# A graph layer's scatter sum on one core: a 256-column window per tile, or 16 slots per tile placed eight tiles at a time

## The chip, the core and the metric

The kernel runs on one core of one Trainium2 chip. The metric is device microseconds of one execution, taken without the profiler; the median of several executions counts. The profile is a separate execution, with the profiler on, and is read for where the time goes. Engines are named as the profile names them: PE is TensorE (PEld is its weight load), DVE is VectorE, ACT is ScalarE, POOL is GpSimd, SP is SyncE.

## What is computed

Two layers of a relational graph convolution over 12,500 nodes with 128 features, 200,000 edges sorted by their destination, and 8 relations. A residual sum and a normalisation over the features follow. Cut to what matters:

```python
def _rgcn_conv(x, src, dst, et, basis, comp, root, bias):
    W = jnp.einsum('rb,bio->rio', comp, basis)
    xw = jnp.einsum('ni,rio->nro', x, W)
    msgs = xw[src, et]                                   # a row for every edge
    seg = dst * N_REL + et
    summed = segment_sum(msgs, seg, N_NODES * N_REL)
    cnt = segment_sum(ones, seg, N_NODES * N_REL)
    mean = summed / jnp.maximum(cnt, 1.0)[:, None]
    agg = mean.reshape(N_NODES, N_REL, HIDDEN).sum(axis=1)
    return agg + x @ root + bias

h = x
for l in range(2):
    h = relu(_rgcn_conv(h, src, dst, et, basis[l], comp[l], root[l], bias[l])) + h
out = layernorm(x + h)
```

## The kernel before

**Tiles, quads and groups.** The 200,000 edges are cut into T = 1563 tiles of 128 edges, in their sorted order. Four tiles make a quad (Q = 4, NQ = 391 quads), eight tiles make a group (G = 8, NG = 196 groups). Nodes go in blocks of 128 (NT = 98 blocks). Because the edges are sorted and the graph has 16 edges for each node on average, a tile's destinations lie within K = 16 neighbouring nodes of the tile's first one, and the destinations of a group of 8 tiles lie in a window of 256 nodes. Where an input does not allow this, a general path behind a branch (line 1287) is taken; it is not taken here.

**Layer 1** (loop at line 1187) gathers the rows of `x` for the edges: `gather`, line 603, one indirect DMA of POOL for each tile, 128 rows of 512 bytes each, four DMAs a quad. `onehot` (line 894) makes for each tile a matrix of 128 edges by 128 columns (8 relations by 16 slots) on DVE: it compares the constant row `cols`, which lies in PSUM, with the edge's own column and multiplies by the edge's weight 1/count. `means` (line 954) multiplies the gathered rows with it, `product` (line 975) applies the 8 relation matrices and leaves 8 tiles x 16 slots = 128 rows of `y`, ACT copies these to `ys` (line 591), and `place` (line 1008) adds them to the window of 256 nodes with a 128x256 matrix of ones and zeros that `place_in` (line 986) makes on DVE from `pos`, the place of every slot. `finish` (lines 1024, 1041, 1042) adds the part carried over from the window before and the bias, applies relu and the residual, and leaves a block of 128 nodes, transposed, in `hT`. `table` (line 1054) multiplies that block with the 8 relation matrices of layer 2 and stores the products to `y_d` in HBM.

**Layer 2** (loop at line 1235) gathers rows of `y_d`, one for each edge, in the same way (line 603, 1563 indirect DMAs of 128 rows). A row is a finished message here, so it is only weighted and summed. `onehot` makes for each tile a matrix of 128 edges by 256 columns, again from `cols`, comparing with `near`, the edge's place in the 256-node window. `add_rows` (line 1091) multiplies the tile's rows, as the stationary operand, with that matrix and accumulates straight into the window of 256 nodes, for about 16 tiles; at the first tile of a window one more matmul adds `h @ root` (line 1094). `finish` then takes the block off, and after every eighth block `norm` turns it back (line 1113), adds `x`, normalises (lines 1119 to 1132) and stores it, in pieces that the list `todo` spreads over the next quads, one piece a quad.

**Order.** No scheduler reorders anything. Each engine executes its instructions in the order of the calls, and the class `Plan` inserts the semaphore waits: a read waits for the write, a new write waits for the readers of the buffer. POOL's queue holds little but the gathers. The gather of quad q + 12 (AHEAD) is issued before quad q is summed, into a ring of 14 buffers (`rows_r`, line 541), so it waits until PE has read quad q - 2; it also waits until the gather three quads earlier has landed (three semaphore lanes, line 571). `onehot` runs two quads ahead in a ring of four (`dm_r`, line 542). The first gather of layer 2 waits for all of `y_d`.

**Preparation.** `counts` (lines 706 to 773) runs once for the first block of 128 tiles before the first quad, and three times for four blocks each during the first quads of layer 1. It makes the tables that `onehot` and `gather` read; `near` is the last of them: one DVE instruction for each block (line 760), transposes on PE (line 767), a copy on ACT.

Of the kernel before, what the change touches and what calls it, by code (L numbers as in the profile page):

```python
# [10 lines left out]
I32 = mybir.dt.int32  # L11
# [404 lines left out]
def ordered_path(  # L416
# [67 lines left out]
    w = keep([P, B * P], F32, "w")  # L484
    near = keep([P, B * P], F32, "near")
    pos = keep([P, B, 2 * R], F32, "pos")
# [40 lines left out]
    def h_cells(j):  # L527
# [7 lines left out]
    small = {n: keep([P, 1], t, n) for n, t in (  # L535
        ("nb_i", I32), ("nb_n", F32), ("p_in", I32), ("p_inf", F32), ("p_g", I32), ("p_gf", F32),
        ("p_r", I32), ("p_rf", F32))}
# [3 lines left out]
    rows_r = Ring(const, AHEAD + 2, [P, Q, D], F32, "rows")  # L541
    dm_r = Ring(const, 4, [P, Q, 2 * P], F32, "dm")
    sT_r = Ring(const, 3, [P, R, G, K], F32, "sT")
# [162 lines left out]
    def counts(i):  # L706
# [51 lines left out]
        nr, nc_ = turns.take()  # L758
        for b in range(b0, b1):
            vec(lambda b=b: nc.vector.tensor_scalar(nr[:, b - b0], dx[:, b, main], small["nb_n"],  # L760
                                                    float(-b * P * G), op0=ALU.subtract, op1=ALU.add),
                dxc + ["nb_n"], [nc_ + (b - b0,)])
        pt, pc = pt_b

        def emit():
            for b in range(nb):
                last = nc.tensor.transpose(pt[:, b, :], nr[:, b, :], ident)
            return last

        pe(emit, [nc_ + (b,) for b in range(nb)] + ["ident"], [pc, nc_])  # L770
        copy(near[:, b0 * P:b1 * P], pt[:, :nb, :].rearrange("p b t -> p (b t)"), [pc],
             [("near", b) for b in range(b0, b1)])
        yield
# [111 lines left out]
    def onehot(l, q):  # L885
        if q >= NQ:
            return
        t, cell = dm_r.take()
        dms[l, q] = (t, cell)
        wide, ids = (P, kr) if l == 0 else (2 * P, near)  # L890

        def emit():
            for i in range(q * Q, q * Q + in_quad(q)):
                last = nc.vector.tensor_scalar(t[:, i - q * Q, :wide], cols[:, :wide], ids[:, i:i + 1],  # L894
                                               w[:, i:i + 1], op0=ALU.is_equal, op1=ALU.mult)
            return last

        b = q * Q // P
        vec(emit, ["cols", ("kr" if l == 0 else "near", b), ("wt", b)], [cell])

# [87 lines left out]

    def place(g):

        m = tiles_of(g) * K
        t, c = pl.pop(g)
        o, oc = ys.pop(g)
        k = two_blocks(g)
        opens = g == 0 or two_blocks(g - 1) != k
        last = g == NG - 1 or two_blocks(g + 1) != k
        if opens:
            b, bc = po_b[k % 2]
            acc[k] = b.rearrange("p t d -> p (t d)")[:, :2 * P], bc
        a, ac = acc[k]  # L1000
        root_in = opens and k >= 0
        reads = [c, oc]
        if root_in:
            xt, xc = x_cols(k)
            reads += xc + [("w", 0, R)]

        def emit():
            ins = nc.tensor.matmul(a, o[:m], t[:m], start=opens, stop=last and not root_in)  # L1008
# [38 lines left out]
    def table(j):  # L1047
# [4 lines left out]
        def half(k):  # L1052
# [12 lines left out]
            elif k == 1:  # L1065
# [7 lines left out]

    acc_b = [(s_b[0][0].rearrange("p t d -> p (t d)")[:, :2 * P], s_b[0][1]),
             (s_b[1][0].rearrange("p t d -> p (t d)")[:, :2 * P], s_b[1][1]),
             (ct_b[0].rearrange("p t d -> p (t d)")[:, :2 * P], ct_b[1])]

    def add_rows(q, k, opens, last):
        t, c = rows_g.pop((1, q))
        d, dc = dms.pop((1, q))  # L1080
        a, ac = acc[k]
        n = in_quad(q)
        root_in = opens and k >= 0
        reads = [c, dc]
        if root_in:
            ht, hc = hT[:, k * P:k * P + rows_of(k)], ("h", k)
            reads += [hc, ("w", 1, R)]

        def emit():
            for i in range(n):  # L1090
                ins = nc.tensor.matmul(a, t[:, i, :], d[:, i, :], start=(opens and i == 0),  # L1091
                                       stop=(last and i == n - 1))
                if i == 0 and root_in:
                    nc.tensor.matmul(a[:, :rows_of(k)], w_sb[:, 1, R, :], ht, start=False, stop=False)
            return ins

        pe(emit, reads, [ac])

    def norm(n, h):
# [4 lines left out]
        xt, xc = xs[n]  # L1104
        b, bc = po_b[h]
        st, sc = st_r.take()
# [34 lines left out]

    def sup(q):
        return (q * Q + G) // (2 * G) - 1


    def run(gen, n):
# [9 lines left out]
    vec(lambda: nc.vector.memset(ones, 1.0), [], ["ones"])  # L1156
    vec(lambda: nc.vector.tensor_single_scalar(small["nb_i"], part, G, op=ALU.add), ["part"], ["nb_i"])
    vec(lambda: nc.vector.tensor_single_scalar(small["nb_i"], small["nb_i"], 4, op=ALU.logical_shift_right), [], ["nb_i"])
    vec(lambda: nc.vector.tensor_copy(small["nb_n"], small["nb_i"]), ["nb_i"], ["nb_n"])
    vec(lambda: nc.vector.tensor_scalar(small["nb_n"], small["nb_n"], float(P), float(-P), op0=ALU.mult, op1=ALU.add),  # L1160
        [], ["nb_n"])
    copy(cols, iota_f, ["iota"], ["cols"])
# [24 lines left out]
    for q in range(NQ - 1):  # L1187
# [8 lines left out]
        if q % 2 == 0:  # L1196
            if g > 0:
                product(g - 1)
        elif g > 0:
            place(g - 1)  # L1200
# [19 lines left out]
    means(NQ - 1)  # L1220
    place(g - 1)
    todo.pop(0)()
    product(g)
    todo.pop(0)()
    place(g)
    while todo:
# [89 lines left out]
```

## Time and profile before

| what | value |
|---|---|
| median of 3 executions | 3990.28 us |
| lowest and highest | 3987.99 us, 3999.04 us |
| profiled execution, its own time | 4626.96 us |
| its span, first to last instruction | 4625.2 us |
| mean granted TensorE clock | 0.741 |
| layer 1: first to last gather | 3.5 to 2333.1 us |
| layer 2: first to last gather | 2378.4 to 4584.9 us |
| PE busy | 2403.7 us, 52% |
| DVE busy | 1652.6 us, 36% |
| ACT busy | 495.7 us, 11% |
| POOL busy | 2962.3 us, 64% |
| DMA engines, mean busy share, from the rows of the 40 slices | 0.1 to 0.3 |

The profiled execution is 637 us longer than the median of the others. A reader has to keep this in mind: a wait that stands in the profile need not stand in an ordinary execution. A line of the table of groups reads: source line, engine, operation, what is written from what, shape, count | busy time and mean of one | idle time of the engine just before such instructions, and what ended most of it. "issue" is idle time that ended without a wait that the profile shows, "remote" idle time ended by something that the profile could not name.

### The profile page before, as it was taken

Reading aid. Unit: us, or ns where it says so; the run is one execution under the profiler, and the core shown is the slowest. Engines: PE = TensorE matmul, PEld = TensorE weight load, DVE = VectorE, ACT = ScalarE, POOL = GpSimd, SP = SyncE. Lnnn points to the kernel's source line nnn. Section 1 sums busy time; section 2 is a strip of 40 time slices with the busy share of each in tenths; the row PEclk is TensorE's granted clock in tenths of the full one; section 3 lists DMA queues with packets and bytes.
Section 4 is the critical chain, followed back from the end, with each engine's and each line's share of the span. In section 5 each row is a group of like instructions: output and inputs, shape, how many; then the busy total and the mean of one; then the engine's idle time right before and its main releaser. Section 6 shows DMA issues by size and latency. Waiting matters only on the chain.

```text
span 4625.2 us, 32936 instructions
## 1 busy us (share of the span) xinstructions
PE 2403.7 (52%) x11205; PEld 1929.6 (42%) x11205; DVE 1652.6 (36%) x4580; ACT 495.7 (11%) x1042; POOL 2962.3 (64%) x3134
## 2 busy tenths in 40 slices
PE   1675655555655655565572454354445453444444
PEld 1454554454545544454452333333333342333333
DVE  3764322222322222222232334343334343333344
ACT  0121211112112212121110000000000000000000
POOL 5466666666666666666646666666666666666664
PEclk9897778777777778777786676666666666676776
DMA  3122222222222222222221121112122121221211
GB/s 85 33 64 73 74 73 69 73 69 73 69 73 74 73 69 74 69 73 66 73 70 45 48 56 55 48 54 57 46 57 55 47 56 45 56 58 45 58 51 38
DMA packets 128275, 282.52 MB, mean 61 GB/s; under 512 B 53327, under 2 KB 60763, under 8 KB 128099
## 3 DMA queue, kind: packets, MB, share of 16 engines
q0 software_dynamic: 100032, 205.07, 17.0%
q1 hardware_dynamic: 25546, 73.59, 4.3%
q10 hardware_dynamic: 2521, 1.66, 0.1%
q8 instruction: 92, 1.51, 0.1%
q14 instruction: 84, 0.69, 0.0%
HBM read 222.51 MB, written 57.60 MB: 61 GB/s over the span
## 4 chain that ended last, share of the span: by engine, by line
another core or an unknown queue 43%; PE 27%; issue 13%; DVE 13%; ACT 3%; POOL 2%; DMA 0%; POOLq 0%; DVEq 0%; ACTq 0%; SPq 0%
DVE dm L894 8%; PE s L954 8%; PE y L975 7%; PE pt L1054 4%; PE po L1008 3%; POOL rows L603 2%; PE ct L1091 2%; ACT sT L591 1%; PE s L1091 1%; PE ct L732 1%; DVE w_sb L623 1%; PE ct L733 1%; DVE arena L726 1%; ACT carry L1024 1%
## 5 line engine op out<-in xcount | busy, mean ns | idle before, releaser
L603 POOL DMA_INDIRECT rows<-in_x_dram,idx x1563 | 1485.2, 950 | 846.9 <-issue 417.3
L603 POOL DMA_INDIRECT rows<-y_d,idy x1563 | 1476.0, 944 | 775.8 <-issue 442.4
L1091 PE MATMUL s<-dm,rows 128*128 128x256 f32 x2086 | 672.0, 479 | 811.2 <-DVE dm L894 518.4
L894 DVE TENSOR_SCALAR dm<-cols,near,w 128x256 f32<-128x256 f32 x1563 | 725.6, 533 | 829.6 <-remote 686.4
L1091 PEld LDWEIGHTS s<-dm,rows 128*128 128x128 f32 x2086 | 491.1, 245 | 958.6 <-DVE dm L894 570.5
L894 DVE TENSOR_SCALAR dm<-cols,kr,w 128x128 f32<-128x128 f32 x1563 | 525.4, 401 | 493.4 <-remote 324.1
L954 PEld LDWEIGHTS s<-dm,rows 128*128 128x128 f32 x3126 | 485.1, 224 | 138.2 <-issue 113.3
L1008 PE MATMUL po<-pl,ys 128*128 128x256 f32 x392 | 168.8, 521 | 698.0 <-ACT ys L591 566.9
L975 PE MATMUL y<-w_sb,sT 128*128 128x128 f32 x3136 | 463.3, 310 | 95.0 <-issue 54.9
L954 PE MATMUL s<-dm,rows 128*128 128x128 f32 x3126 | 492.9, 307 | 20.4 <-issue 19.2
L1091 PE MATMUL ct<-dm,rows 128*128 128x256 f32 x1040 | 334.2, 478 | 325.2 <-DVE dm L894 187.0
L975 PEld LDWEIGHTS y<-w_sb,sT 128*128 128x128 f32 x3136 | 442.8, 225 | 110.7 <-issue 63.4
L1091 PEld LDWEIGHTS ct<-dm,rows 128*128 128x128 f32 x1040 | 245.9, 245 | 395.5 <-DVE dm L894 213.3
L1008 PEld LDWEIGHTS po<-pl,ys 128*128 128x128 f32 x392 | 74.3, 237 | 728.9 <-ACT ys L591 590.4
L1041 DVE TENSOR_TENSOR v<-po,carry 128x128 f32<-128x128 f32 x98 | 28.5, 291 | 932.2 <-ACT carry L1024 782.3
L591 ACT ACTIVATE sT<-s 128x512 f32<-128x512 f32 x391 | 233.7, 598 | 758.3 <-PE s L954 412.6
L1054 PE MATMUL pt<-w_sb,arena 128*128 128x512 f32 x388 | 239.8, 705 | 21.0 <-issue 8.9
L1024 ACT ACTIVATE carry<-s,bias_t 128x128 f32<-128x128 f32 x65 | 23.9, 368 | 1321.4 <-remote 1026.3
L591 ACT ACTIVATE y_row<-pt 128x512 f32<-128x512 f32 x194 | 115.7, 596 | 258.9 <-PE pt L1054 80.9
L591 ACT ACTIVATE ys<-y 128x128 f32<-128x128 f32 x196 | 54.2, 277 | 756.0 <-remote 526.8
L732 PE MATMUL ct<-arena,id_h 128*128 128x512 f16 (+1 forms) x188 | 70.9, 397 | 94.4 <-DVE arena L726 65.4
L1041 DVE TENSOR_TENSOR v<-s,carry 128x128 f32<-128x128 f32 x66 | 18.9, 286 | 274.8 <-ACT carry L1024 152.4
(121 smaller groups left out, 978.2 us busy)
## 6 DMA issues: line engine op xcount, KB each, us to landing
y_d<-y_row SPq DMA_DIRECT2D x96, 512.0 KB
rows<-in_x_dram,idx POOLq DMA_INDIRECT x1563
rows<-y_d,idy POOLq DMA_INDIRECT x1563
x_g<-in_x_dram SPq DMA_DIRECT2D x24, 512.0 KB
out_dram<-x_g SPq DMA_DIRECT2D x12, 512.0 KB
arena<-in_L_gnn_basis_dram SPq DMA_DIRECT2D x2, 512.0 KB
arena<-in_dst_dram ACTq DMA_DIRECT2D x2, 448.0 KB
arena<-in_edge_type_dram SPq DMA_DIRECT2D x2, 448.0 KB
```

The lines of the kernel that those rows point to most:

```text
L591: act(lambda: nc.scalar.activation(out_t, in_t, AF.Copy), reads, writes)
L603: return [nc.gpsimd.indirect_dma_start(out=t[:, i - q * Q, :], out_offset=None, in_=x if l == 0 else y_d, in_offset=bass.IndirectOffsetOnA ...
L623: vec(lambda b=b: nc.vector.scalar_tensor_tensor(w_sb[:, l, r, :], b_sb[:, l, b, :], comp_sb[:, c0 + b:c0 + b + 1], w_sb[:, l, r, :], op0= ...
L732: nc.tensor.matmul(ct[:, :nb, :], id_h, eq[:, s - s0, :nb, main], start=(s == 1), stop=False)
L894: last = nc.vector.tensor_scalar(t[:, i - q * Q, :wide], cols[:, :wide], ids[:, i:i + 1], w[:, i:i + 1], op0=ALU.is_equal, op1=ALU.mult)
L954: last = nc.tensor.matmul(s[:, i, :], t[:, i, :], d[:, i, :P], start=True, stop=True)
L975: last = nc.tensor.matmul(y[:m], t[:, r, :nt, :].rearrange("p t k -> p (t k)"), w_sb[:, 0, r, :], start=(r == 0), stop=(r == R - 1))
L1008: ins = nc.tensor.matmul(a, o[:m], t[:m], start=opens, stop=last and not root_in)
L1024: act(lambda: nc.scalar.activation(nt, a[:, P:], AF.Identity, bias=bias_t[:, l:l + 1]), [ac, ("bias_t", l)], [ncell])
L1041: vec(lambda: nc.vector.tensor_add(v[:, :n], a[:, :n], t[:, :n]), [ac, c], [vc])
L1054: pe(lambda: nc.tensor.matmul(hb[:n].rearrange("p r d -> p (r d)"), hT[:, j * P:j * P + n], w_sb[:, 1, k * H:(k + 1) * H, :].rearrange("p ...
L1091: ins = nc.tensor.matmul(a, t[:, i, :], d[:, i, :], start=(opens and i == 0), stop=(last and i == n - 1))
```

## The change

Layer 2 sums as layer 1 does, in two steps in place of one. `onehot` makes a matrix of 32 columns for each tile in place of 256: it compares with `slot`, the distance of the edge's destination from the tile's first destination, plus 16 for tiles of odd number. `sums` takes the place of `add_rows`: now the 32-column matrix is the stationary operand and the gathered rows (128 columns) are the moving one; two neighbouring tiles accumulate into the same 32 partitions, one using the first 16 and the other the last 16, so that 8 tiles fill 128 partitions of a PSUM bank (`y` for even groups, the first quarter of `ct` for odd ones). After the second quad of a group ACT copies the bank to `ys`. `place_in` makes the matrix of places as in layer 1, and `place`, which now takes the layer as an argument, adds the group's 128 slots to the window of 256 nodes one group later, in the banks `po`, with the root's matmul at the opening of a window. `norm` takes the banks `s` in place of `po`. What followed the last `add_rows` of a window (`finish`, and the start of `norm`) follows `place` now. In `counts`, `slot` is made with two DVE instructions for all blocks of a call (a subtraction of two arrays, then an addition of `odd`) in place of one instruction for each block.

The number of matmuls for the sum itself stays at one for each tile. Gathers, their order and the rings' depths are the same; `dm_r` has half the width.

```diff
@@ -533,13 +533,13 @@
...
-    dm_r = Ring(const, 4, [P, Q, 2 * P], F32, "dm")
+    dm_r = Ring(const, 4, [P, Q, P], F32, "dm")
...
@@ -756,20 +756,11 @@
         turned("DVE", idy, "idy", iy, ic, b0, b1)
         yield
         nr, nc_ = turns.take()
-        for b in range(b0, b1):
-            vec(lambda b=b: nc.vector.tensor_scalar(nr[:, b - b0], dx[:, b, main], small["nb_n"],
-                                                    float(-b * P * G), op0=ALU.subtract, op1=ALU.add),
-                dxc + ["nb_n"], [nc_ + (b - b0,)])
-        pt, pc = pt_b
-
-        def emit():
-            for b in range(nb):
-                last = nc.tensor.transpose(pt[:, b, :], nr[:, b, :], ident)
-            return last
-
-        pe(emit, [nc_ + (b,) for b in range(nb)] + ["ident"], [pc, nc_])
-        copy(near[:, b0 * P:b1 * P], pt[:, :nb, :].rearrange("p b t -> p (b t)"), [pc],
-             [("near", b) for b in range(b0, b1)])
+        vec(lambda: nc.vector.tensor_tensor(nr[:, :nb], dx[:, bs, main],
+                                            dx[:, bs, HALO:HALO + 1].to_broadcast([P, nb, P]), op=ALU.subtract),
+            dxc, [nc_])
+        vec(lambda: nc.vector.tensor_scalar(nr[:, :nb], nr[:, :nb], small["odd"], None, op0=ALU.add), ["odd"], [nc_])
+        turned("ACT", slot, "slot", nr, nc_, b0, b1)
         yield
 
     def where():
...
@@ -887,16 +878,16 @@
             return
         t, cell = dm_r.take()
         dms[l, q] = (t, cell)
-        wide, ids = (P, kr) if l == 0 else (2 * P, near)
+        m, ids = (P, kr) if l == 0 else (2 * K, slot)
 
         def emit():
             for i in range(q * Q, q * Q + in_quad(q)):
-                last = nc.vector.tensor_scalar(t[:, i - q * Q, :wide], cols[:, :wide], ids[:, i:i + 1],
+                last = nc.vector.tensor_scalar(t[:, i - q * Q, :m], cols[:, :m], ids[:, i:i + 1],
                                                w[:, i:i + 1], op0=ALU.is_equal, op1=ALU.mult)
             return last
 
         b = q * Q // P
-        vec(emit, ["cols", ("kr" if l == 0 else "near", b), ("wt", b)], [cell])
+        vec(emit, ["cols", ("kr" if l == 0 else "slot", b), ("wt", b)], [cell])
 
 
     def shape_of(n):
...
@@ -986,7 +977,7 @@
...
-    def place(g):
+    def place(l, g):
...
@@ -1001,20 +992,20 @@
         root_in = opens and k >= 0
         reads = [c, oc]
         if root_in:
-            xt, xc = x_cols(k)
-            reads += xc + [("w", 0, R)]
+            xt, xc = x_cols(k) if l == 0 else (hT[:, k * P:k * P + rows_of(k)], [("h", k)])
+            reads += xc + [("w", l, R)]
 
         def emit():
             ins = nc.tensor.matmul(a, o[:m], t[:m], start=opens, stop=last and not root_in)
             if root_in:
-                ins = nc.tensor.matmul(a[:, :rows_of(k)], w_sb[:, 0, R, :], xt, start=False, stop=last)
+                ins = nc.tensor.matmul(a[:, :rows_of(k)], w_sb[:, l, R, :], xt, start=False, stop=last)
             return ins
 
         pe(emit, reads, [ac])
         if last:
-            n = finish(0, k)
+            n = finish(l, k)
             if n is not None:
-                table(k)
+                table(k) if l == 0 else norms(k)
 
     def finish(l, k):
 
...
@@ -1071,30 +1062,36 @@
     todo = []
 
 
-    acc_b = [(s_b[0][0].rearrange("p t d -> p (t d)")[:, :2 * P], s_b[0][1]),
-             (s_b[1][0].rearrange("p t d -> p (t d)")[:, :2 * P], s_b[1][1]),
-             (ct_b[0].rearrange("p t d -> p (t d)")[:, :2 * P], ct_b[1])]
-
-    def add_rows(q, k, opens, last):
+    sum_b = [y_b, ct_b]
+
+    def sums(q):
         t, c = rows_g.pop((1, q))
         d, dc = dms.pop((1, q))
-        a, ac = acc[k]
+        g = q * Q // G
+        y, yc = sum_b[g % 2]
+        y = y if g % 2 == 0 else y[:, 0, :]
         n = in_quad(q)
-        root_in = opens and k >= 0
-        reads = [c, dc]
-        if root_in:
-            ht, hc = hT[:, k * P:k * P + rows_of(k)], ("h", k)
-            reads += [hc, ("w", 1, R)]
 
         def emit():
             for i in range(n):
-                ins = nc.tensor.matmul(a, t[:, i, :], d[:, i, :], start=(opens and i == 0),
-                                       stop=(last and i == n - 1))
-                if i == 0 and root_in:
-                    nc.tensor.matmul(a[:, :rows_of(k)], w_sb[:, 1, R, :], ht, start=False, stop=False)
-            return ins
-
-        pe(emit, reads, [ac])
+                j = (q * Q + i) % G // 2 * 2 * K
+                last = nc.tensor.matmul(y[j:j + 2 * K, :], d[:, i, :2 * K], t[:, i, :], start=(i % 2 == 0),
+                                        stop=(i % 2 == 1 or i == n - 1))
+            return last
+
+        pe(emit, [c, dc], [yc])
+        if q % 2 == 1 or q == NQ - 1:
+            m = tiles_of(g) * K
+            o, oc = ys[g] = ys_r.take()
+            copy(o[:m], y[:m], [yc], [oc])
+
+    def norms(k):
+        n = k // S
+        if k % S == S - 1 or k == NT - 1:
+            for h in range(-(-shape_of(n)[1] // 4)):
+                norm(n, h)
+            if n + 2 < NX:
+                todo.append(lambda: load_x(n + 2))
 
     def norm(n, h):
 
...
@@ -1102,7 +1099,7 @@
...
-        b, bc = po_b[h]
+        b, bc = s_b[h]
...
@@ -1233,26 +1225,20 @@
     for q in range(2):
         onehot(1, q)
     for q in range(NQ):
-        k = sup(q)
+        g = q * Q // G
         gather(1, q + AHEAD)
         if q + AHEAD == NQ - 1:
             pool(lambda: nc.gpsimd.drain())
         onehot(1, q + 2)
-        opens = q == 0 or sup(q - 1) != k
-        last = q == NQ - 1 or sup(q + 1) != k
-        if opens:
-            acc[k] = acc_b[k % 3]
-        add_rows(q, k, opens, last)
+        if q % 2 == 0 and g > 0:
+            place_in(g - 1)
+        sums(q)
+        if (q % 2 == 1 or q == NQ - 1) and g > 0:
+            place(1, g - 1)
         if todo:
             todo.pop(0)()
-        if last:
-            finish(1, k)
-            n = k // S
-            if k >= 0 and (k % S == S - 1 or k == NT - 1):
-                for h in range(-(-shape_of(n)[1] // 4)):
-                    norm(n, h)
-                if n + 2 < NX:
-                    todo.append(lambda n=n: load_x(n + 2))
+    place_in(NG - 1)
+    place(1, NG - 1)
     while todo:
         todo.pop(0)()
 
```

More of the change, by code (lines that the diff above doesn't have):

```diff
@@ L484, in ordered_path @@
     w = keep([P, B * P], F32, "w")
-    near = keep([P, B * P], F32, "near")
+    slot = keep([P, B * P], F32, "slot")
     pos = keep([P, B, 2 * R], F32, "pos")
@@ L535, in ordered_path @@
     small = {n: keep([P, 1], t, n) for n, t in (
-        ("nb_i", I32), ("nb_n", F32), ("p_in", I32), ("p_inf", F32), ("p_g", I32), ("p_gf", F32),
+        ("odd_i", I32), ("odd", F32), ("p_in", I32), ("p_inf", F32), ("p_g", I32), ("p_gf", F32),
         ("p_r", I32), ("p_rf", F32))}
@@ L1140, in norm @@
         todo.extend([add, stats, scale] + ([store] if h == (k - 1) // 4 else []))
-    def sup(q):
-        return (q * Q + G) // (2 * G) - 1
     def run(gen, n):
@@ L1156, in ordered_path @@
     vec(lambda: nc.vector.memset(ones, 1.0), [], ["ones"])
[L1157 to L1161, printed above, removed]
+    vec(lambda: nc.vector.tensor_single_scalar(small["odd_i"], part, 1, op=ALU.bitwise_and), ["part"], ["odd_i"])
+    vec(lambda: nc.vector.tensor_copy(small["odd"], small["odd_i"]), ["odd_i"], ["odd"])
+    vec(lambda: nc.vector.tensor_scalar(small["odd"], small["odd"], float(K), None, op0=ALU.mult), [], ["odd"])
     copy(cols, iota_f, ["iota"], ["cols"])
@@ L1199, in ordered_path @@
         elif g > 0:
-            place(g - 1)
+            place(0, g - 1)
             k, n = two_blocks(g - 1), two_blocks(g - 1) // S + 1
@@ L1220, in ordered_path @@
     means(NQ - 1)
-    place(g - 1)
+    place(0, g - 1)
     todo.pop(0)()
@@ L1224, in ordered_path @@
     todo.pop(0)()
-    place(g)
+    place(0, g)
     while todo:
```

## The prediction

> **What bounds the kernel now.** I read the page's table of groups first, then the waits of the gathers' line, then the busy times of equal stretches of the two layers, then the order of time in layer 2.
>
> ```profile
> L603 POOL DMA_INDIRECT rows<-in_x_dram,idx x1563 | 1485.2, 950 | 846.9 <-issue 417.3
> L603 POOL DMA_INDIRECT rows<-y_d,idy x1563 | 1476.0, 944 | 775.8 <-issue 442.4
> L894 DVE TENSOR_SCALAR dm<-cols,near,w 128x256 f32<-128x256 f32 x1563 | 725.6, 533 | 829.6 <-remote 686.4
> L894 DVE TENSOR_SCALAR dm<-cols,kr,w 128x128 f32<-128x128 f32 x1563 | 525.4, 401 | 493.4 <-remote 324.1
> L1008 PE MATMUL po<-pl,ys 128*128 128x256 f32 x392 | 168.8, 521 | 698.0 <-ACT ys L591 566.9
> ```
>
> The gathers are 3126 equal instructions. POOL is busy 2961 us with them and idle 1623 us before them. The waits of line 603 split that idle time:
>
> ```profile
>   issue: 859.7, 2800
>   remote: 468.7, 163
>   PE s L954: 191.7, 84
>   DMA y_d<-y_row: 44.4, 1
> ```
>
> "issue" is 0.30 us for a step from one gather to the next. The other waits, small ones included, are 319 and sum to some 755 us; less the 0.3 us that each would have had anyway, POOL really stood still for about 755 - 319 x 0.3 = 659 us. That is nearly the 637 us by which the profiled execution (4626.96 us) exceeds the median (3990.28 us).
>
> The order of time in layer 2 shows what a stop looks like:
>
> ```profile
> 3024.27 1.99 PE L1091 MATMUL s<-dm,rows 128*128 128x256 f32 x8 [0.55 <-issue]
> ...
> 3028.08 3.19 PE L1091 MATMUL ct<-dm,rows 128*128 128x256 f32 x14
> ...
> 3031.72 0.95 POOL L603 DMA_INDIRECT rows<-y_d,idy  x1 [0.31 <-issue]
> 3032.97 0.94 POOL L603 DMA_INDIRECT rows<-y_d,idy  x1 [0.30 <-issue]
> ...
> 3038.62 0.37 ACT L1024 ACTIVATE carry<-s,bias_t 128x128 f32<-128x128 f32 x1 [15.86 <-remote]
> 3039.03 0.29 DVE L1041 TENSOR_TENSOR v<-s,carry 128x128 f32<-128x128 f32 x1 [9.95 <-issue]
> ```
>
> The last matmul into `s` ends at 3026.3, yet ACT, which waits for it alone, starts at 3038.6; DVE stands behind ACT, and PE behind DVE's next one-hot. PE, DVE and ACT are idle together while POOL goes on at 1.25 us a gather. Neither throughput nor data explains those 12 us[...]. I take these delays to be the recorder's, since the ordinary execution has no room for them: from 3017.99 to 3050.46 there are 26 steps of POOL, 1.249 us each; 3126 x 1.249 = 3904 us, and 86 us remain of the median. Real waits claim those: 3.5 us before the first gather, the stop before the first quads are summed (22.5 + 29.5 us in the profile), 44.4 us for `y_d`, 41 us from the last gather's end (4585.9) to the end. They sum to 141 us, more than is left, so even these are shorter ordinarily, or the pace is a little faster (1% is 39 us). POOL's pace is the bound in both layers; PE (busy 44 to 48% of the layer-2 stretches), DVE (32 to 39%), ACT (2%) and DMA (at most 0.2) are not.
>
> [...] gathers are 1.25 us apart while DVE works (3021.7 to 3029) and while it is idle (3029 to 3039). So a cheaper one-hot doesn't speed the gathers. [...]
>
> **The change part by part**, against the profiled execution, in which the gathers alone take 3904 of 4627 us; a step hidden behind them is hidden in both, so the differences carry over to the median.
>
> *One-hot.* 128 columns cost 401 ns, 256 cost 533: 1.03 ns a column, so 32 cost about 302 ns. 1563 x 231 ns = 361 us of DVE's busy time go. Cover: the gathers; a quad takes POOL 5.0 us, and DVE has four one-hots, 1.9 us before, and some 0.6 us of `finish` and `norm`. Worth 0; the other bound is in the faster rival.
>
> *Sum.* The moving operand shrinks from 256 to 128 columns. By the rows of lines 1091 and 954, a tile is two matmul records of 479 ns before and of about 307 after: 1563 x 2 x 172 = 538 us of PE's modelled busy time go. A load of 32 columns is not in the trace; between nothing and the 245 ns of a full load, I take no gain. All beside POOL: 0.
>
> *Placing.* Added for each of 196 groups: `place_in` 473 ns on DVE (93 us in all), a copy to `ys` 277 ns on ACT (54 us), two matmul records of 521 ns on PE (204 us). Each quad of layer 2 then has PE about 2.5 + 0.5 us, DVE 1.2 + 0.24 + 0.6, ACT 0.14 and a little: all under 5.0 us. New waits: PE's `place` of group g - 1 waits for ACT's copy, with the next group's sums in front of it and the quad after behind it. The copy was asked for a group, 10 us, earlier. Behind a late `place` stand the sums, and behind them, through the row buffers, the gathers; these have 12 quads, 60 us, of slack. Cost 0; its other bound is the slower rival.
>
> *Preparation.* 13 instructions of 281 ns (line 760) become four subtractions (298 ns for one block as at line 819, 682 for four as at line 740) and four additions (237 and, by line 748's 685 as a ceiling, up to 685): at most +0.25 us in the serial start, +0.25 us for each later call; one tiny setup instruction goes. I take +0.5 us. POOL's, SP's and the DMA queues' instructions are the same and in the same order.
>
> *End.* Here nothing covers. Before, the last quad's matmuls start at 4606.4 and DVE's last instruction ends at 4613.6: 7.2 us. After, sums of three tiles (0.8), then in PE order `place` of group 194 (0.6). Then DVE in its order: v and wide of block 96 (0.29 + 0.29), the addition of the block-11 half (0.68), `place_in` of group 195 (0.47), v and wide of block 97 (0.21 + 0.25), the half's statistics (0.86 + 0.36, ACT's 0.5 with its hops), reciprocal and scaling (0.17 + 1.12), then the last block's addition, statistics and scaling (0.42 + 0.79 + 0.5 + 0.17 + 0.6): 7.7, with the front 9.1. Waits between engines, seven more or so of 0.1 to 0.2 us, raise it to about 10.3. The step behind: one piece of `todo` fewer is done before the last landing, since `norm` of block 11 enters the list two quads later. Added: about 3 us; bounds 1 and 8.
>
> Sum: 0 + 0 + 0 + 0.5 + 3 = +3.5 us. 3990.3 + 3.5 = **3994 us**.
>
> **Rivals.**
>
> *Slower: late hand-overs are real in ordinary executions too.* The change adds one hand-over PE to ACT to PE for each group, and layer 1 shows its price: line 1008 is idle 566.9 us until `ys` comes. Gathers in stretches of 400 us:
>
> ```profile
> 800.00:1200.00 400.00, 235.70 (x1306) 201.69 (x1305) 116.84 (x356) 78.49 (x160) 263.08 (x279) 0.78 0.24 71
> 1600.00:2000.00 400.00, 228.52 (x1318) 193.35 (x1318) 112.77 (x344) 79.72 (x162) 263.62 (x280) 0.79 0.25 72
> 2800.00:3200.00 400.00, 182.08 (x616) 141.72 (x615) 148.12 (x376) 7.75 (x22) 267.22 (x284) 0.69 0.19 52
> 3600.00:4000.00 400.00, 190.16 (x617) 145.26 (x618) 155.25 (x384) 7.83 (x22) 264.31 (x281) 0.67 0.19 51
> ```
>
> Over all such stretches layer 1 has 278.75 gathers and layer 2 283.2 (fifth pair of numbers: POOL's busy time and count): 1.435 against 1.412 us. If layer 2 takes layer 1's pace, 1563 x 0.023 = 36 us: **4030 us**. It decides once the delays use up the 60 us of slack, so that POOL waits for PE. For: in the profile they do. Against: the 86 us.
>
> *Faster: some of layer 2's stops are real, and shorter PE and DVE work removes them.* POOL's ordinary pace could be 1.20 us; then 3126 x 1.20 = 3751, 239 us remain, about 100 over the 141 above, and layer 2 has some 45 of these: **3949 us**. For: PE and DVE do less. Against: the stops are not busy time, and the profile shows no faster pace.
>
> That the new path does less than it says I exclude: by the code the same tiles are summed and placed.
>
> **How the numbers follow.** A measurement of this kernel tells 0.3%, 12 us, from no change. The forecast, no measurable change, has 0.51; the slower rival, with an end longer than I bound it, 0.29; the faster 0.20. The likeliest case's own range is 3985 to 4000. To leave out no more than 2 in 10, the range goes to 3950 below and to 4038 above, a little past the slower rival.
>
> **What would show it.** In the new profile: gathers still 1.25 us apart; one-hot near 0.30 us; 392 new records of placing in layer 2, near 0.52 us each, whose idle time ends with `ys`; DVE's last instruction about 10 us after the last quad's first matmul. If POOL's step changes, or an ordinary time moves by over 12 us, then stops in layer 2 are part of ordinary executions and I am wrong.

## The result and the profile after

| what | before | after |
|---|---|---|
| median of 14 executions | 3990.18 us | 3997.89 us |
| lowest and highest | 3986.98 us, 3999.04 us | 3993.59 us, 4003.6 us |
| profiled execution, its own time | 4626.96 us | 3997.74 us |
| its span | 4625.2 us | 3996.0 us |
| mean granted TensorE clock | 0.741 | 0.675 |
| PE busy | 2403.7 us | 2093.2 us |
| DVE busy | 1652.6 us | 1378.5 us |
| ACT busy | 495.7 us | 565.7 us |
| POOL busy | 2962.3 us | 2961.9 us |

The ratio is 1.002, 95% interval [1.0011, 1.0028]: 7.7 us more, where 3.5 were forecast. By the bound of 0.3%, the 12 us that the executions of before lie apart, this is no change. The interval leaves out 1, so the small loss is real, and it is surely not a gain.

One thing has to be seen first. The profiled execution of the changed kernel took 3997.74 us, in the middle of its other executions, and has none of the stops that filled the profile of before. The two profiles therefore must not be subtracted from each other: their 629 us of difference are not the change. What can be read is the profile after by itself, against the durations that the prediction gave.

Groups of the changed kernel (line, engine, operation, what is written from what, count | busy us, mean ns of one | idle us just before, and what ended most of it):

```profile
L603 POOL DMA_INDIRECT rows<-in_x_dram,idx x1563 | 1485.9, 951 | 514.8 <-issue 440.8
L603 POOL DMA_INDIRECT rows<-y_d,idy x1563 | 1474.9, 944 | 493.1 <-issue 464.8
L885 DVE TENSOR_SCALAR dm<-cols,slot,w 128x32 f32<-128x32 f32 x1563 | 374.7, 302 | 501.9 <-PE y L1078 494.2
L1078 PE MATMUL y<-rows,dm 128*32 128x128 f32 x1568 | 210.7, 419 | 642.2 <-DMA rows<-y_d,idy 642.2
L1078 PEld LDWEIGHTS y<-rows,dm 128*32 128x32 f32 x1568 | 119.2, 158 | 756.0 <-issue 396.7
L999 PE MATMUL po<-pl,ys 128*128 128x256 f32 (+1 forms) x784 | 370.4, 567 | 12.2 <-DVE pl L977 9.5
L977 DVE TENSOR_SCALAR pl<-cols,pos 128x256 f32<-128x256 f32 x392 | 186.0, 475 | 0.0
```

The gathers are as they were, and their idle time is now nearly all "issue". The sums of layer 2 start after a wait for a gather (642.2 of 642.2 us): PE stands ready and POOL is late. That is what a kernel bound by POOL looks like from PE's side.

The waits of the gathers' line, idle us and times, and then who waited for the gathers:

```profile
  issue: 905.6, 2971
  PE s L945: 45.1, 26
  DMA rows<-in_x_dram,idx: 22.6, 74
  DMA y_d<-y_row: 17.1, 1
...
  PE y L1078: 642.2, 196
  PE ct L1078: 592.5, 195
```

There is no "remote" line any more, and POOL waits for no matmul of layer 2. The whole span can be laid out: 3.4 us to the first gather, 1998.3 us for the gathers of layer 1, 18.1 us to the first of layer 2, 1950.0 us for those of layer 2, and 26.1 us from the last gather's start to the end.

The same core in two stretches of 400 us, one in each layer (busy us and count for PE, PEld, DVE, ACT, POOL, then the granted clock, DMA share, GB/s):

```profile
400.00:800.00 400.00, 273.01 (x1500) 229.59 (x1499) 133.19 (x403) 93.53 (x185) 302.42 (x321) 0.82 0.28 82
...
2800.00:3200.00 400.00, 147.39 (x788) 86.95 (x790) 116.91 (x484) 20.23 (x66) 302.41 (x321) 0.50 0.22 61
```

321 gathers start in either layer, 1.249 us from one to the next, against 279 and 283 on average in such stretches of the profile of before. In layer 2 PE is busy 37% and DVE 29% of the time. The granted clock there is 0.50, where it was 0.66 to 0.70. PE is busy for less of the time and is also granted a lower clock; that the one brings the other is not shown.

The two layers put 392 placing records each into the line of L999 above, and its mean of 567 ns mixes them. By the trace it is 419 ns in layer 1 and 714 ns in layer 2. Most of layer 2 by itself:

```profile
L999 PE MATMUL po<-pl,ys 128*128 128x256 f32 x373 | 228.0, 715 | 0.0
```

The end of the changed kernel, in order of time (start us, duration us, engine and line, what, and in brackets the idle time before and what ended it):

```profile
3969.82 0.94 POOL L603 DMA_INDIRECT rows<-y_d,idy  x1 [0.30 <-issue]
...
3973.01 1.06 PE L1078 MATMUL ct<-rows,dm 128*32 128x128 f32 x6 [1.79 <-DMA rows<-y_d,idy]
3973.99 1.22 PE L999 MATMUL po<-pl,ys 128*128 128x256 f32 x2
...
3975.26 0.37 ACT L1015 ACTIVATE carry<-po,bias_t 128x128 f32<-128x128 f32 x1 [0.87 <-PE po L999]
3975.66 0.29 DVE L1032 TENSOR_TENSOR v<-po,carry 128x128 f32<-128x128 f32 x1 [7.56 <-ACT carry L1015]
...
3976.79 0.47 DVE L977 TENSOR_SCALAR pl<-cols,pos 48x256 f32<-48x256 f32 x1
3977.31 1.22 PE L999 MATMUL po<-pl,ys 48*128 48x256 f32 x2 [1.24 <-DVE pl L977]
...
3978.46 0.72 PE L1001 MATMUL po<-arena,w_sb 128*128 128x84 f32 x2
3979.22 0.25 DVE L1032 TENSOR_TENSOR v<-po,carry 128x84 f32<-128x84 f32 x1 [1.96 <-PE po L1001]
...
3979.66 0.87 DVE L1120 BATCH_NORM_STATS2 st<-x_g 128x6 f32<-128x128 f32 x4
...
3984.15 0.60 DVE L1129 TENSOR_SCALAR x_g<-x_g,st 106x128 f32<-106x128 f32 x2
```

The same two points in the profile of before:

```profile
4606.44 0.60 PE L1091 MATMUL s<-dm,rows 128*128 128x256 f32 x2
...
4613.01 0.60 DVE L1132 TENSOR_SCALAR x_g<-x_g,st 106x128 f32<-106x128 f32 x2
```

From the last quad's first matmul (3973.01) to the end of DVE's last instruction (3984.75) pass 11.7 us, where the kernel before had 7.2 (4606.4 to 4613.6). DVE has been idle 7.56 us at 3975.66, although what follows there includes work that needs nothing of the last quad. The two ends are not alike, however: here PE waits 1.79 us for the last quad's rows, in the profile of before it comes to them late, 21.5 us after the last gather's start.

### The profile page after: what moved, and what is told of

It is laid out like the page before. It is cut to its first block, busy times and chain, and to the rows that moved or that the text cites. A ratio compares the mean times of both kernels' runs of the same rounds, so it can differ in the third digit from the quotient of the medians.

```text
span 3996.0 us, 33928 instructions
## 1 busy us (share of the span) xinstructions
PE 2093.2 (52%) x11597; PEld 1548.1 (39%) x11597; DVE 1378.5 (34%) x4770; ACT 565.7 (14%) x1238; POOL 2961.9 (74%) x3134
## 4 chain that ended last, share of the span: by engine, by line
POOL 54%; issue 29%; DMA 7%; PE 4%; DVE 4%; ACT 0%; POOLq 0%; ACTq 0%; DVEq 0%; SPq 0%
POOL rows L603 54%; DMA rows<-in_x_dram,idx 5%; DMA rows<-y_d,idy 2%; PE s L945 1%; PE y L966 1%; DVE w_sb L623 1%; PE ct L732 1%; DVE dm L885 1%; PE ct L733 1%; DVE arena L726 1%; PE pt L1045 0%; PE pt L689 0%; DMA arena<-in_dst_dram 0%; PE po L999 0%; DVE arena L749 0%
## 5 line engine op out<-in xcount | busy, mean ns | idle before, releaser
L945 PEld LDWEIGHTS s<-dm,rows 128*128 128x128 f32 x3126 | 454.2, 220 | 720.8 <-DMA rows<-in_x_dram,idx 554.3
L885 DVE TENSOR_SCALAR dm<-cols,slot,w 128x32 f32<-128x32 f32 x1563 | 374.7, 302 | 501.9 <-PE y L1078 494.2
L1078 PE MATMUL y<-rows,dm 128*32 128x128 f32 x1568 | 210.7, 419 | 642.2 <-DMA rows<-y_d,idy 642.2
L1078 PE MATMUL ct<-rows,dm 128*32 128x128 f32 x1558 | 209.6, 419 | 592.5 <-DMA rows<-y_d,idy 592.5
L1078 PEld LDWEIGHTS y<-rows,dm 128*32 128x32 f32 x1568 | 119.2, 158 | 756.0 <-issue 396.7
L1078 PEld LDWEIGHTS ct<-rows,dm 128*32 128x32 f32 x1558 | 119.5, 158 | 666.6 <-issue 423.0
L999 PE MATMUL po<-pl,ys 128*128 128x256 f32 (+1 forms) x784 | 370.4, 567 | 12.2 <-DVE pl L977 9.5
L591 ACT ACTIVATE ys<-y 128x128 f32<-128x128 f32 (+1 forms) x294 | 81.4, 277 | 1118.5 <-PE y L1078 759.5
L999 PEld LDWEIGHTS po<-pl,ys 128*128 128x128 f32 (+1 forms) x784 | 163.9, 261 | 89.5 <-issue 79.7
L977 DVE TENSOR_SCALAR pl<-cols,pos 128x256 f32<-128x256 f32 x392 | 186.0, 475 | 0.0
```

Source lines behind the costliest of these rows:

```text
L591: act(lambda: nc.scalar.activation(out_t, in_t, AF.Copy), reads, writes)
L885: last = nc.vector.tensor_scalar(t[:, i - q * Q, :m], cols[:, :m], ids[:, i:i + 1], w[:, i:i + 1], op0=ALU.is_equal, op1=ALU.mult)
L945: last = nc.tensor.matmul(s[:, i, :], t[:, i, :], d[:, i, :P], start=True, stop=True)
L977: vec(lambda: nc.vector.tensor_scalar(t[:m], cols[:m], pos[:m, g // (2 * R), g % (2 * R):g % (2 * R) + 1], None, op0=ALU.is_equal), ["cols ...
L1078: last = nc.tensor.matmul(y[j:j + 2 * K, :], d[:, i, :2 * K], t[:, i, :], start=(i % 2 == 0), stop=(i % 2 == 1 or i == n - 1))
```

## Experiments

The questions were where the 7.7 us come from, and whether the prediction's reasons (gathers set the pace; everything else is beside them; the end is bare) hold or only happened to give a near number. On the two chips where these kernels ran, the kernel before took about 4632 us in its timed executions as well, not 3990; on which chip the first executions ran is not known. So each ratio below is against the kernel before on the same chip: 4633.67 us for the first four runs, 4631.31 for the next four, 4632.32 for the last four. The ratios and their intervals are an estimate of their own; the quotients of the medians lie up to 0.0015 from them.

### The kernel before again, and once more

No edit.

> The kernel before, profiled once more. Theory (the gathers' pace on POOL is the bound, the stops in the first profile were the recorder's): where the recorder does not stop it, the span is about 3990 us, gathers stand 1.25 us apart in both layers, POOL's waits other than issue sum to about 60 us (start and the change of layers) and not 755 us. Rival (the stops belong to the kernel): POOL's other waits are again several hundred us and the profiled span is again far over 3990 us. It also gives the undisturbed end of the kernel before, from the last quad's first matmul to DVE's last instruction, which the prediction took as 7.2 us from a disturbed one.

> The kernel before once more, for its trace on this chip. If the chip is one without stops: span about 3988 us, POOL's waits other than issue about 60 us, the end from the last quad's first matmul to DVE's last instruction 6 to 7 us. If it is one with stops: as in the second profile, 750 us of such waits.

4631.98 us and, on the other chip, 4631.27 us, each in the one execution that was profiled. The waits of the gathers' line in the first of the two:

```profile
  issue: 860.1, 2799
  remote: 480.4, 165
  PE s L954: 202.2, 90
  DMA y_d<-y_row: 44.4, 1
```

These are the stops of the profile of before, each sum within 12 us (859.7, 468.7, 191.7, 44.4). But here they are also in the time of the timed executions: 21 of the kernel before on this chip lie between 4625.59 and 4643.66 us. So the stops are not a thing of one separate profiled execution. The prediction called them the recorder's; as it put it, that is not borne out.

### The changed kernel again

No edit.

> The changed kernel as it is, beside the one with the other end. Theory (the end alone, about +5, and a little at the start): on a chip where gathers run without stops (the kernel before near 3990 us) a ratio of 1.002, on one with the stops (near 4634 us) a difference of +5 to +13 us. Slower rival (the added hand-over prolongs the stops): on a chip with stops +36 us or more.

> The changed kernel once more, as the reference of the three beside it. Its ratio to the kernel before was 1.0020 on the first chip and 1.0022 on another: both theories expect 1.001 to 1.003 again (+4 to +12 us). Theory A (the buffers' places or the program set the step of the gathers): if its timed runs are near 4639, the median step between two gathers that no stop parts is 1.251 to 1.252 us, the gather itself 947 ns. Theory B (only the longer end and preparation): 1.249 and 944, as in the kernel before.

4638.89 us, ratio 1.0022 [1.0011, 1.0033], and 4643.85 us, ratio 1.0023 [1.0013, 1.0033]. The change costs the same 0.2% with the stops as without them. The slower rival (36 us, if late hand-overs are real) had its best ground here, where the hand-overs are late, and does not appear: a gather of layer 2 takes 1.4157 us on average with the change and 1.4146 without. The faster rival (some 45 us to gain, if shorter work of PE and DVE removes stops) does not appear either. In the two profiles the tail from the last gather's start to the end is 45.7 us in both; in the kernel before it was 40.1 and 40.8 us.

### More work for DVE in layer 2

Each one-hot of layer 2 of the kernel before is made twice, or three times, the repeats into an unused buffer.

```diff
+    idle_r = Ring(const, 1, [P, Q, 2 * P], F32, "idle")
...
+        for _ in range(1 if l == 1 else 0):        # 2 in the second kernel
+            u, uc = idle_r.take()
...
+                    last = nc.vector.tensor_scalar(u[:, i - q * Q, :], cols, ids[:, i:i + 1],
+                                                   w[:, i:i + 1], op0=ALU.is_equal, op1=ALU.mult)
```

> The kernel before, each one-hot of layer 2 made twice (the second into a buffer that nothing reads). DVE has then about 3.7 + 0.6 us a quad in layer 2, POOL's gathers 5.0. Theory (hidden behind the gathers): no change within 5 us of 3990 us, though DVE gets 700 us more to do; so taking 361 us away is worth nothing either. Rival (DVE's work in layer 2 shows in the time): 3990 plus a good part of 700 us; even a tenth would give 4060 us.

> The kernel before, each one-hot of layer 2 made three times. DVE has then about 3 x 1.85 + 0.6 = 6.1 us a quad, more than POOL's 5.0. Theory: now DVE is the bound in layer 2 and the time grows by about 391 x 1.1 = 430 us, less some 60 us that the row buffers take up at most: 4360 to 4450 us. If it stays under 4050 us, the theory's size for the cover is wrong.

Twice: 4651.06 us, ratio 1.0053 [1.0035, 1.0071]. Three times: 4812.31 us in one execution. A stretch of layer 2 in the kernel before, then with two and with three one-hots for each tile (columns as above):

```profile
2800.00:3200.00 400.00, 179.98 (x590) 138.44 (x591) 148.35 (x376) 7.76 (x22) 265.55 (x282) 0.68 0.19 52
```

```profile
2800.00:3200.00 400.00, 204.58 (x619) 147.38 (x619) 279.48 (x665) 7.65 (x22) 266.38 (x283) 0.74 0.19 52
```

```profile
2800.00:3200.00 400.00, 221.31 (x579) 154.00 (x580) 385.53 (x887) 6.86 (x20) 252.31 (x267) 0.67 0.18 49
```

With two, DVE is busy 279 us in place of 148, and POOL still does 283 gathers: layer 2 takes 2212.1 us from first to last gather, against 2209.6. Some 700 us of additional DVE work (2360 against 1654 us busy) vanish beside the gathers. So the 351 us that the change takes from DVE's one-hots could not bring anything. The time grew by 17 us by the medians, where at most 5 were expected. 14 us of that are in the end, where nothing covers the repeats: the tail from the last gather's start is 54.0 us, against 40.1.

With three, DVE is busy 386 of 400 us and is the bound: 2333.6 us for 391 quads, 5.97 us a quad, near the 6.1 expected. The whole grew by 179 us and not by the 430 expected, because that was counted from 3990 us, without stops. Layer 2 grew by 124 us, from 2209.6 us that already had the stops in them, and the tail by 50 us, to 89.8. So the new bound first takes the place of the stops.

### Three gathers a quad

Layer 2 of the kernel before gathers and sums only three of a quad's four tiles; every fourth tile is left out of layer 2, its one-hot is still made.

```diff
-                for i in range(q * Q, min((q + 1) * Q, T))]
+                for i in range(q * Q, min(q * Q + (Q if l == 0 else 3), T))]
...
-        n = in_quad(q)
+        n = min(3, in_quad(q))
```

> The kernel before with three gathers a quad in layer 2 in place of four: it leaves out every fourth tile of layer 2's sum, so the output is not the reference's. Theory (POOL's pace is the bound): on a chip without stops 391 x 1.249 = 488 us less, about 3500 us. On a chip with stops PE's late completions are the bound of layer 2, and the gain is smaller: with three quarters of the matmuls between stops as well, anything from 250 to 500 us less than 4634. Rival (gathers are not the bound in either): less than 100 us.

4080.19 us in one execution, 551 us less. Layer 2 has 390 gathers fewer and takes 1658.7 us for 1172 steps: 1.4153 us a gather, stops included. The kernel before has 1.4146 on these chips (2209.6 / 1562) and the changed one 1.4157. 390 x 1.415 = 552. The time of layer 2 goes with the number of gathers and with nothing else that was tried short of a saturated DVE, and so do the stops. The miss is in the expectation: it took the stops to be a fixed amount.

### The end reordered

In the changed kernel, for the last quad, the matrix of places of the last group, the placing of the group before and all postponed pieces are issued ahead of the last sums.

```diff
+        if q == NQ - 1:
+            place_in(NG - 1)
+            place(1, g - 1)
+            while todo:
+                todo.pop(0)()
...
-        if (q % 2 == 1 or q == NQ - 1) and g > 0:
+        if q % 2 == 1 and g > 0:
...
-    place_in(NG - 1)
```

> The changed kernel with another order at its end alone: for the last quad, the matrix of places of the last group, the placing of the group before it and all outstanding pieces of normalisation are issued before the last quad's sums. Theory (the change costs only what it adds after the last landing): DVE's last instruction comes about 7 us after the last quad's first matmul, not 11.7, so the median falls by 4 to 5 us, to about 3993 us; what then is left over the kernel before is 2 to 4 us. Rival (the 7.7 us lie in layer 2's course, in the added hand-over of each group): no change, 3998 us.

> The changed kernel with the end reordered, on the same chip as the changed kernel. Theory: 4 to 5 us less than the changed kernel (DVE's last instruction some 7 us after the last quad's first matmul, not 11.7). Rival (the cost is not at the end): the same as the changed kernel within 2 us.

4640.95 us, ratio 1.0018 [1.0011, 1.0025], and 4640.37 us, ratio 1.0021 [1.0013, 1.003]: nothing that can be told from the changed kernel itself. The theory of both expectations missed, and the rival's number came. The end of the changed kernel with stops, in order of time:

```profile
4597.83 0.94 POOL L603 DMA_INDIRECT rows<-y_d,idy  x1 [0.30 <-issue]
4602.15 0.28 ACT L591 ACTIVATE ys<-ct 128x128 f32<-128x128 f32 x1 [20.80 <-remote]
...
4602.72 0.29 DVE L1032 TENSOR_TENSOR v<-po,carry 128x128 f32<-128x128 f32 x1 [19.41 <-ACT carry L1015]
...
4604.66 1.22 PE L999 MATMUL po<-pl,ys 128*128 128x256 f32 x2 [16.95 <-DVE pl L977]
...
4619.90 1.06 PE L1078 MATMUL ct<-rows,dm 128*32 128x128 f32 x6
...
4631.68 0.60 DVE L1129 TENSOR_SCALAR x_g<-x_g,st 106x128 f32<-106x128 f32 x2
```

PE waits for DVE, DVE for ACT and ACT for something that no record names, 17 to 21 us, past the last gather. Some nine quads are still to be summed then, so the last quad starts at 4619.90, when PE comes to it, and not when its rows land. The last quad of the reordered kernel (the run with the wide ring, below):

```profile
4617.99 1.06 PE L1078 MATMUL ct<-rows,dm 128*32 128x128 f32 x6
...
4624.67 0.60 DVE L1129 TENSOR_SCALAR x_g<-x_g,st 106x128 f32<-106x128 f32 x2
```

From the first matmul to DVE's end it now takes 7.3 us in place of 12.4 (7.2 and 8.1 in the two reordered kernels above), so the edit does what it should. But the work that it brought forward stands in a queue that is behind anyway: the last quad starts 24.7 to 26.1 us after the last gather's start in place of 21.1 to 22.1, and the tails (43.8 and 45.7 us, 43.0 in the last run) differ from the 45.7 by less than 3 us. Where the last quad waits for its rows, as at 3973.01 above with 1.79 us of PE idle, the moved work would fall into a gap. That was not measured: no chip of these experiments was without stops. The rival named another place, layer 2's course. Against it stand layer 2's own lengths: 1950.0 us in the changed kernel's first profile, which is 1562 steps of 1.248 us, and on the chips with stops 1.6 us more than before.

### Where the buffers lie, and the pace of the gathers

In the profiles of the eight runs so far a gather took 944 ns in the kernel before (median, and in its version with three gathers a quad) and 947 in all others, changed kernels and repeated one-hots alike; the step in layer 2 was 1.249 against 1.251 us. 0.002 us for 3126 gathers are 6 us, which would explain most of 7.7. The changed kernel's first profile already stood against it, with 944 ns and 1.249 us. The theory (A below): the narrower ring, or the additional one, moves all buffers behind it, and the gather's speed hangs on that. Three kernels, beside the changed kernel itself; the third is the wide ring with the reordered end:

```diff
 # changed kernel, wide ring
-    dm_r = Ring(const, 4, [P, Q, P], F32, "dm")
+    dm_r = Ring(const, 4, [P, Q, 2 * P], F32, "dm")
 # kernel before, padded
     dm_r = Ring(const, 4, [P, Q, 2 * P], F32, "dm")
+    keep([P, 1024], F32, "pad")
```

> The changed kernel, with the ring of stationaries kept at the width that it had before (256 columns a tile, of which layer 2 now writes 32), so that every buffer after it lies where it lay before. Nothing else differs. Theory A (places in SBUF set the gather's 944 or 947 ns): step back to 1.249, 3126 gathers by 0.002 to 0.003 us less, 6 to 9 us less than the changed kernel beside it, so 1.000 to 1.001 of the kernel before. Theory B (places are nothing, the +7.6 is the end and the preparation): the same as the changed kernel, 1.002, step unchanged.

> The kernel before, with an unused buffer of 4 KB in each partition laid behind the ring of stationaries, as the two kernels with repeated one-hots had one. The instructions are the same. Theory A: the step becomes 1.251 to 1.252 and the time 6 to 9 us more, 1.0013 to 1.002. Theory B, and a rival by which it is the program and not the buffers' places that sets the step: no change, 0.9995 to 1.0005, step 1.249.

> The changed kernel with the wide ring and, for the last quad, the placing of the slots before and all postponed norms and stores issued ahead of its sums. Theory A: 1.000 or a little under; the reordered end gained nothing measurable by itself (1.0018 and 1.0021 against 1.0022), so no more than 2 us less than the wide ring alone. Theory B: 1.002.

Wide ring: 4642.01 us, ratio 1.0023 [1.0014, 1.0032]. Padded: 4633.93 us, ratio 1.0005 [0.9996, 1.0013]. Wide ring and reordered end: 4641.09 us, ratio 1.0017 [1.0008, 1.0026]. The theory falls. The wide ring did have 944 ns and a step of 1.249 us, but not the shorter time, and with the reordered end it had 947 ns and 1.251 us. The step is no property of the change either. For the changed kernel, two profiles on one chip (minimum, median and maximum ns, first and last start):

```profile
L603 POOL DMA_INDIRECT rows<-y_d,idy x1563: 940/947/992, 2383.1 to 4594.3; - x196
```

```profile
L603 POOL DMA_INDIRECT rows<-y_d,idy x1563: 938/944/1028, 2386.6 to 4597.8; - x196
```

The same kernel has 947 once and 944 the other time, and the run with 944 was not the shorter one (4643.85 against 4638.89 us). The 3 ns go with a run, not with the change.

## Why the prediction was right, point by point

**The gathers' pace is the bound: right, and shown from three sides.** POOL's steps, where no stop parts them, are 1.249 us with and without the change; doubled DVE work does not move layer 2 (2212.1 us against 2209.6); a quarter of the gathers less takes a quarter of layer 2 away (1658.7 us).

**A cheaper one-hot does not speed the gathers: the runs agree.** With three one-hots for each tile and DVE 97% busy in layer 2, the step between gathers that no stop parts (steps under 1.4 us) had a mean of 1.2510 us, and in the changed kernel, with DVE a quarter busy on chips with stops too, 1.2483 and 1.2505; in the kernel before it is 1.249.

**The stops are the recorder's: not borne out as it was put.** What it was used for held: an execution of 3990 us has no room for the stops, so a step hidden behind the gathers is worth nothing. The changed kernel's own profile shows the rest. The waits that the prediction added up to 141 us, and said had to be shorter, are 3.4 + 46.4 + 17.1 + 25.2 = 92 us there: the first gather, what the steps over 1.4 us in layer 1 exceed 1.249 us by, the wait for `y_d`, and the end from the last gather's end. With the 3904 us of gathers that is the span. But on the chips of the experiments the stops are in timed executions too, and the changed kernel's first profile has none, so "profiled or ordinary execution" was the wrong division. The chip could be the right one, if the first profile came from another chip than the three executions beside it; that is not known and was not tested. What ACT waits for in a stop, no record names. That the recorder makes the stops was an estimate, from the 659 us of POOL's standing still against the 637 us of difference; what makes them is shown by no run here and stays open. Two of the prediction's sums here are a little off: its 755 us are the nine largest waits without "issue", and all of them come to 763; its 41 us after the last gather run to the execution's own 4626.96 us, and to the end of the span they are 39.3.

**One-hot: right.** 302 ns from a line through two widths; measured 302. Busy time fell by 351 us, worth nothing.

**Sum: the worth right, the duration not.** A record takes 419 ns, not 307, at a granted clock of 0.50, not 0.7; the load of 32 columns, left open between nothing and 245 ns, takes 158. Records overlap, though (3126 of 419 ns, end to end, would be 1310 us), so the busy time is the better measure: for these matmuls it fell from 672 + 334 = 1006 us to 211 + 210 = 420, by 586, where 538 were put. Before, and after (the line of `y` stands above):

```profile
L1091 PE MATMUL s<-dm,rows 128*128 128x256 f32 x2086 | 672.0, 479 | 811.2 <-DVE dm L894 518.4
L1091 PE MATMUL ct<-dm,rows 128*128 128x256 f32 x1040 | 334.2, 478 | 325.2 <-DVE dm L894 187.0
```

```profile
L1078 PE MATMUL ct<-rows,dm 128*32 128x128 f32 x1558 | 209.6, 419 | 592.5 <-DMA rows<-y_d,idy 592.5
```

Hidden all the same: PE is 37% busy.

**Placing: the worth right, the matmuls too small, and wrong in what they wait for.** `place_in` 475 ns (473), the copy 277 (277), but a matmul record of layer 2 takes 714 ns (521): 240 us in all where 204 were put. And `place` hardly waits at all: 12.2 us before 784 records of both layers, and 9.5 of these for the matrix of places, none for `ys`. The 566.9 us that layer 1's `place` waited for `ys` in the profile of before were the stops. With them the slower rival's premise goes: layer 1 is not slower than layer 2 when there are none (321 gathers in 400 us in both).

**End: the mechanism right, the size too small.** About 3 us were put for it, from 7.2 to 10.3; it took 11.7, so +4.5, inside the bounds of 1 and 8. Its waits between engines, 1.2 us in all, were an estimate; at the end of the profile after, such a wait takes 0.03 to 0.05 us, as from ACT's end at 3975.63 to DVE's start at 3975.66. What the sum left out is the last group's `place`. It counts that of group 194, but between `place_in` of group 195 and the next instruction of DVE lie two more placing records and the root's matmul: DVE is idle 1.96 us until 3979.22 while PE works on them from 3977.31. The kernels with stops say the same: 45.7, 45.7 and 44.9 us of tail with the change (the last with the wide ring), 40.1, 40.8 and 41.3 without (the last padded), means 4.7 apart. In these six the last quad starts 21.1 to 22.1 us after the last gather's start, whichever the kernel; from there to DVE's end pass 12.4 us with the change and 7.3 without. How long the end of the kernel before is when its last quad waits for its rows, no profile shows, so on a chip without stops the +4.5 is an estimate.

**Preparation: not settled.** 0.5 us were put, and the time of this part alone was not measured. Of the 7.7 us the end leaves some 3 if its 4.5 hold. Layer 2 from first to last gather took 2211.2 to 2211.5 us in six profiles with the new sums and 2209.6 to 2210.0 in three of before on these chips: 1.6 us, of a cause that I don't know. What remains is about 1.6 us, less than layer 1 differs between profiles of one kernel (2329.2 and 2331.7 us in the kernel before on these chips).

## What to carry to other kernels

When one engine's instructions follow each other at one step for the whole run, as the 3126 gathers 1.249 us apart do here, count them and multiply by their step before anything else; work that was taken from other engines beside them was worth nothing here, because it changed neither that count nor that step. What such a change still can alter are the ends where nothing covers: there the second stage was paid (the tails grew by 4.7 us), and every instruction of it between two engines has to stand in the sum. And where the queue is behind at the end, an order mended there only moved work from one place to another here (tails of 43.0 to 45.7 us against 45.7); whether it pays where the queue waits was not measured.

## What the runs showed of the hardware

- The same kernel takes 3990 us in some executions and 4632 in others. Between its stops the step of the gathers is 1.249 us, as in the changed kernel's profile without stops. The stops (in the profile of before POOL waits 163 times for what no record names, 2.9 us on average and 9.8 at most) part the gathers so that one of layer 2 takes 1.415 us on average, whatever PE and DVE have to do (1.4146, 1.4157, 1.4153 and, with doubled one-hots, 1.4162 in four kernels), until DVE is saturated (1.494, with DVE busy 386 of 400 us).
- The granted TensorE clock in layer 2 is lower with the narrow matmuls, with stops or without: 0.53 and 0.50, against 0.66 to 0.70 with the wide ones. A record of half the width took 419 ns in place of 479, but PE's busy time in these records fell from 1006 to 420 us: the mean duration of one record does not tell what a stream of them costs. In the same layer a placing record, with 256 columns to move, took 714 ns, and in layer 1, at a clock of 0.82 in the stretch shown above, 419.
- One-hots of 32 columns last 302 ns each, but four take 0.96 us: they overlap, and start 0.22 us apart.
